# A float32 convolution with a mixing layer on one core: the last row of each output tile from four column products, two sums moved to accumulating DMA, the norms' steps listed singly

## The chip, the core and the metric

The program runs on one core of a Trainium2 chip. The core has TensorE (PE: matrix products, results in PSUM), VectorE (DVE), ScalarE (ACT), GpSimd (POOL, which here only issues DMAs that add into their destination) and SyncE (SP, which issues the plain loads and stores). The metric is the device time of one execution in microseconds; a lower time is better. A float32 product of a 128x128 weight with 512 columns shows as two matmul instructions in the profile.

## The reference

```python
def reference(x, g_pos, g_neg, bias, input_factor, output_factor, Wq, Wk, Wv, B, Wm):
    x = x + conv(groupnorm(x))        # layer 0
    x = x + mix(groupnorm(x))         # layer 1
    return x                          # x: 16 x 128 x 64 x 64, float32

def conv(x):
    v = round(clip(x * input_factor, -1, 1) * 127) / 127 * 0.6
    v = pad(swapaxes(v, -2, -1), 1)
    fv = v + 0.1 * v ** 3
    outs = [conv3x3(fv, g_pos[i] - g_neg[i]) for i in range(3)]     # 128 -> 128 channels
    adc = lambda y: clip(round(y * 0.01 * 256) / 256, -16, 16)
    m = adc(outs[2]) + 4 * adc(outs[0]) + 2 * adc(outs[1]) + adc(outs[2])
    return transpose(m * output_factor + bias)

def mix(x):                           # x as (channels, 4096)
    q, k, v = Wq @ x, Wk @ x, Wv @ x  # 64 rows each
    num, den = exp(B) @ (exp(k) * v), exp(B) @ exp(k)
    return Wm @ (q * num / den)
```

groupnorm works on 32 groups of 4 channels. The three convolutions of a 64x64 image are nearly all of the work.

## The kernel before, in words

The 16 images follow each other. For each image the convolution is done by three blocks, one for each weight set `i`, and each block by two halves: the steps of an image are numbered `.0` to `.5`, with `.0`, `.2`, `.4` the even halves (h = 0) and `.1`, `.3`, `.5` the odd ones (h = 1).

The rows of an image are cut into 16 tiles of four output rows. The 3x3 convolution over such a tile uses a short-convolution scheme down the rows with six points: each point is a fixed combination of input rows, multiplied with a fixed combination of weight rows, and the products are combined to the four output rows. Points 1 to 4 are the inner ones; points 0 and 5 touch only output row 0 and output row 3. Along a row the scheme takes pairs of columns: even columns `ev` and odd columns `od` lie side by side in a row of 66 entries.

**Inner points (class `Block`, `half`).** An even half makes points 1 and 2, an odd half points 3 and 4, with the same steps for each point (u = 0 or 1). There are four column products per point, each a 128x128 weight out of `us` with 512 columns: `q1` (weight 1 with `cs`, the sum of odd and even columns, into `pa`), an ACT copy `m1` of that to `d`, `q2` (weight 2 with `cq`, their difference, added in `pa`), an ACT copy `sd` with the sign turned from `pa` to `pb`, `q0` (weight 0 with a part of `cd`, neighbouring differences, added in `pa`), `q3` (weight 3 with another part of `cd`, added in `pb`), and an ACT copy `sA` of `pa` to `s`. VectorE then does `Bo` (s[1] = 2 d + pb), `df` (d = s[1] - s[0]) and the sum `sm`: in an even half a DMA from POOL adds s[0] into s[1]; in an odd half VectorE does it, doubled, by a custom operation (`doubled_sum`).

**Output rows (`rest`, numbered one higher than the half whose results they use).** `ma` and `mc` write output rows 1 and 2 by a custom operation that adds, bounds and rounds to int16 (`add_bounded`); `mc` reads both sums. `S0` and `S3` combine the point sums for rows 0 and 3 on VectorE. Rows 0 (even half) and 3 (odd half) also need point 0 or 5, and that goes directly: `P` is a product of weight 0 of `ud` with `sv` (sums of pairs of columns) into py[1], `bc` copies py[1] to py[0] on ACT, and `o0` and `o1` add two products each with windows of `v` into py[0] and py[1]. `tk` then adds py and the combined sums, bounded, to int16. `aA` and `aB` add the block's int16 result to `acc`: for block 0 a doubling on VectorE, for the others an adding DMA.

**Input steps of the next image** lie among these: `li`, `lj` (loads), `sx`, `sy` (sums for the norm), the norm, `n`, `cl`, `s`, `va` (quantise, clip, square, value), `cp`, `gr`, `er` (row combinations), `pa`, `pb` (inner points), `cs`, `cq`, `cd` (their columns), `p0`, `e0` (point 0 and its `sv`), `p5`, `e5` (point 5 and its `sv`). A norm is eight steps, `0 a pm b pv c l d`, with the prefix x or y; `a`, `b`, `c` and `d` are runs of small VectorE instructions on 128x1 data that are issued as a block. **Steps of the image before**: `cx` (acc to x2), `cd0x` to `cd3x` (POOL adds the input to x2), `sq`, the y norm, and the mixing layer on four chunks: `xn`, `kp`, `vp`, `qp`, `ek`, `ekv`, `dn`, `g`, `u`, `ln`, `ex`, `oa`, `ob`, `oc`, `op`, `r`, then `rd` (POOL adds x2) and `st` (store).

Every engine works its instructions strictly in the order of issue. That order is written out by hand in three lists: `FIRST` for the weights and images 0 and 1, `ORDER` for images 2 to 14, `LAST` for image 15 and the end; "+1" means the step of the image one turn before. There is no other scheduling; waits come from data alone. Weight preparation (`W0a` to `W2p`) lies in `FIRST`.

`L551` is the helper `mm` through which all convolution products go; `L558` is `add_bounded`; `L561` the doubled sum; `L588` is `Bo`, `L589` is `df`, `L597` the sum by DMA, `L615` and `L618` are `S0` and `S3`, `L624` is `bc`, `L640` the adding DMA into acc, `L697` that of the input, `L808` that of `rd`, `L509` to `L511` the columns, `L520` the pairs, `L745`, `L755`, `L767` the matmuls of the mixing layer, `L804` and `L805` are `ob` and `oc`, `L783` is the add of the last image's mixing output.

Of the kernel before, what the change touches and what calls it, by code (L numbers as in the profile page):

```python
# [39 lines left out]
    cl0+1 q01.2+1 S3.2+1 q00.2+1 sq2+1 tk.2+1 cl1+1 cd0x+1 sA1.2+1 q31.2+1 q11.3+1 s0+1 sA0.2+1  # L40
    m11.3+1 va0+1 q30.2+1 s1+1 q21.3+1 q10.3+1 sq1+1 m10.3+1 P.3+1 q20.3+1 Bo.2+1 sd1.3+1 q01.3+1
    va1+1 df.2+1 lj2+1 sq3+1 lj3+1 gr0+1 sd0.3+1 st3+1 sq0+1 q31.3+1 q30.3+1 sA1.3+1 bc.3+1 q00.3+1
    ya+1 Bo.3+1 sA0.3+1 pmy+1 yb+1 o0.3+1 n2+1 pvy+1 er0+1 st2+1 n3+1 yc+1 o1.3+1 q10.4+1 yl+1 cl2+1
    yd+1 xn0+1 q11.4+1 sm.2+1 tk.3+1 df.3+1 kp0+1 cp+1 vp0+1 m11.4+1 P.4+1 cl3+1 ma.4+1 m10.4+1
    aB.3+1 q20.4+1 ek0+1 bc.4+1 s3+1 ekv0+1 sd0.4+1 dn0+1 sm.3+1 mc.4+1 va3+1 q21.4+1 s2+1 g0+1 li0
    sx0 xn1+1 li1 S0.4+1 u0+1 ln0+1 sd1.4+1 oa0+1 x0 o0.4+1 o1.4+1 q30.4+1 ex0+1 tk.4+1 vp1+1 ob0+1
    qp0+1 kp1+1 oc0+1 aA.2+1 op0+1 va2+1 ek1+1 r0+1 ekv1+1 gr1+1 q01.4+1 sx1 q31.4+1 q00.4+1 sA0.4+1
    P.5+1 S3.4+1 sA1.4+1 bc.5+1 q10.5+1 Bo.4+1 q11.5+1 rd0+1 df.4+1 m10.5+1 er1+1 dn1+1 sy0 g1+1
    u1+1 sm.4+1 o0.5+1 o1.5+1 oa1+1 m11.5+1 st0+1 q21.5+1 aA.4+1 ln1+1 q20.5+1 pa0+1 tk.5+1 ex1+1
    sd1.5+1 pb0+1 q01.5+1 ob1+1 sd0.5+1 q00.5+1 cq0+1 xn2 qp1+1 q30.5+1 q31.5+1 oc1+1 cd0+1 cs0+1  # L50
    Bo.5+1 op1+1 sA0.5+1 kp2 r1+1 li2 vp2 q10.0 ek2 sA1.5+1 P.0 bc.0 q11.0 ekv2 pa1+1 o0.0 m11.0
# [11 lines left out]
    hs0+2 hs2+2 x0+2 hs3+2 hq0+2 hq2+2 hi+2 hq1+2 hs1+2 hq3+2 xa+2 pmx+2 xb+2 pvx+2 xc+2 xl+2 xd+2  # L63
    hn3+2 hn2+2 hc2+2 hn1+2 hn0+2 W2a+2 W1a+2 W0a+2 hc0+2 hc3+2 hc1+2 W0A+2 hr1+2 hr0+2 hv1+2 hv0+2
    gr0+2 W1A+2 er0+2 hr2+2 W0b+2 li0+1 hv2+2 W0j+2 cp+2 W0c+2 W0f+2 W0e+2 W0d+2 W0g+2 W0i+2 W0h+2
    hr3+2 li1+1 W0J+2 W0n+2 hv3+2 W0l+2 er1+2 sx0+1 W0m+2 W1c+2 x0+1 hz1+2 gr1+2 hcq1+2 W1b+2 pa1+2
    hcs1+2 hcd1+2 W2A+2 W1j+2 sx1+1 W0p+2 sy0+1 W0o+2 q10.0+1 sy1+1 li3+1 hz0+2 li2+1 W1e+2 W2b+2
    hcs0+2 W2c+2 m10.0+1 p0+1 sx3+1 pb1+2 q11.0+1 sx2+1 m11.0+1 q20.0+1 hcq0+2 W1f+2 q21.0+1 sy2+1
    cd1+2 sy3+1 hcd0+2 W1J+2 sd0.0+1 xa+1 sd1.0+1 q01.0+1 sA1.0+1 W1d+2 cs1+2 pmx+1 lj0+1 W2J+2
    q31.0+1 cq1+2 q00.0+1 q30.0+1 xb+1 pvx+1 q11.1+1 W1g+2 sA0.0+1 W1h+2 e0+1 Bo.0+1 m11.1+1 q10.1+1  # L70
    m10.1+1 W2d+2 W1i+2 W2e+2 q20.1+1 W1l+2 lj1+1 xc+1 W1m+2 W2g+2 sd0.1+1 df.0+1 q21.1+1 W2j+2 xl+1
    W0k+2 P.2+1 sm.0+1 sd1.1+1 q00.1+1 xd+1 W1n+2 q01.1+1 W1o+2 W2f+2 bc.2+1 sA0.1+1 p5+1 W2h+2
    q31.1+1 n0+1 q10.2+1 W1p+2 q30.1+1 sA1.1+1 W2i+2 cl0+1 Bo.1+1 m10.2+1 q20.2+1 W2m+2 sd0.2+1 n1+1
    o0.2+1 q11.2+1 W1k+2 q00.2+1 m11.2+1 df.1+1 sm.1+1 q30.2+1 q21.2+1 e5+1 ma.2+1 mc.2+1 S0.2+1
# [886 lines left out]
```

## Time and profile before

| | |
|---|---|
| median of 3 runs | 1575.94 us (1574.69 to 1576.45) |
| the profiled execution | 1571.91 us, its span 1570.1 us |
| instructions | 14797 |
| matmuls py<-v (points 0 and 5) | 760 instructions, 363.1 us |
| matmuls py<-sv | 192 instructions, 100.7 us |
| VectorE doubled sum 128x1024 | 48 x 1227 ns |
| POOL's sum by DMA | 48 issues, 512 KB each, 855 ns |
| DMA | 227.01 MB, 145 GB/s in the mean |

The profile's page gives the busy time of each engine over the span, a row of 40 slices with the busy share in tenths, and groups of like instructions: engine, operation, output<-inputs, shape, count, busy time, mean duration in ns, then the idle time of the engine ahead of them and what ended it. A stretch of time can be asked for by itself, with busy times of all engines. A line of waits has the waiting engine and line, what released it, the total in us, how often, and the longest.

### The profile page before, as it was taken

To read this page: it belongs to the slowest core of one execution; us is meant where nothing else is said; L and a number is where in the kernel's file an instruction comes from. 1 tells how busy PE (TensorE), PEld (TensorE's weight loads), DVE (VectorE), ACT (ScalarE), POOL (GpSimd) and SP (SyncE) were. 2 spreads that over 40 slices of the span, in tenths; PEclk is the share of its full clock that TensorE was granted. 3 is DMA by queue.
4 is the path that set the end of the run, shared out by engine and by line. 5 is a ranking of instruction groups with operands and counts; after the bars stand their busy time and mean duration, and the time that the engine had idled before them with its cause. 6 is when DMAs were issued, how large, how long until landed. Compare 5 with 4: busy or idle time off the path is not lost.

```text
span 1570.1 us, 14797 instructions
## 1 busy us (share of the span) xinstructions
PE 1481.1 (94%) x4684; PEld 564.2 (36%) x4684; DVE 1427.7 (91%) x1817; ACT 1115.6 (71%) x1859; POOL 223.1 (14%) x254
## 2 busy tenths in 40 slices
PE   1589999999999999999999999999999999999996
PEld 0233333333333433333343333433333333333331
DVE  4999999999999999999999999999999999998774
ACT  4655868687686868768686776968678686865654
POOL 2001011120201112011121201112020111201120
PEclk6799999999999999999999999999999999999997
DMA  6226478484756848476593847759385774835375
GB/s 175 78 70 132 111 165 195 107 183 134 153 147 153 209 90 181 138 155 161 131 208 98 174 137 164 173 115 219 96 168 141 165 183 108 195 87 121 81 128 154
DMA packets 67359, 227.01 MB, mean 145 GB/s; under 512 B 7632, under 2 KB 8272, under 8 KB 67280
## 3 DMA queue, kind: packets, MB, share of 16 engines
q0 software_dynamic: 38480, 125.52, 43.2%
q1 hardware_dynamic: 28512, 99.50, 18.4%
q10 hardware_dynamic: 288, 1.05, 0.2%
q8 instruction: 37, 0.61, 0.2%
q14 instruction: 42, 0.34, 0.1%
HBM read 102.30 MB, written 33.55 MB: 87 GB/s over the span
## 4 chain that ended last, share of the span: by engine, by line
PE 51%; DVE 28%; ACT 10%; issue 6%; DMA 5%; DVEq 0%; POOL 0%; ACTq 0%; POOLq 0%
PE py L551 15%; PE pa L551 14%; PE pb L551 7%; PE pz L745 5%; DVE y L558 5%; PE py L767 4%; DVE d L589 3%; DVE acc L558 3%; ACT gs L359 3%; PE py L745 3%; DVE s L615 3%; PE pz L755 2%; DMA x<-in_x_dram 2%; DVE f L502 2%; DVE s L561 2%
## 5 line engine op out<-in xcount | busy, mean ns | idle before, releaser
L551 PE MATMUL py<-v,ud 128*128 128x512 f32 x760 | 363.1, 610 | 0.0
L551 PE MATMUL pa<-cs,us 128*128 128x512 f32 x384 | 195.1, 611 | 34.2 <-DVE us L327 33.1
L551 PE MATMUL pb<-cd,us 128*128 128x512 f32 x384 | 192.7, 609 | 12.4 <-ACT pb L582 10.5
L551 PE MATMUL pa<-cq,us 128*128 128x512 f32 x384 | 197.1, 616 | 4.1 <-ACT d L580 3.9
L551 PEld LDWEIGHTS py<-v,ud 128*128 128x128 f32 x760 | 137.5, 189 | 170.4 <-issue 149.3
L551 PE MATMUL pa<-cd,us 128*128 128x512 f32 x384 | 194.6, 609 | 3.6 <-DVE x L363 2.5
L582 ACT ACTIVATE pb<-pa 128x512 f32<-128x512 f32 x192 | 112.4, 585 | 66.6 <-PE pa L551 61.6
L580 ACT ACTIVATE d<-pa 128x512 f32<-128x512 f32 x192 | 110.8, 594 | 44.1 <-PE pa L551 31.0
L808 POOL DMA_DIRECT2D xn<-x x58 | 50.2, 870 | 607.5 <-ACT xn L778 600.3
L585 ACT ACTIVATE s<-pa 128x512 f32<-128x512 f32 x192 | 111.0, 594 | 35.6 <-PE pa L551 29.8
L588 DVE SCALAR_TENSOR_TENSOR s<-d,pb 128x1024 f32<-128x1024 f32 x96 | 116.6, 1215 | 5.7 <-PE pb L551 5.6
L589 DVE TENSOR_TENSOR d<-s 128x1024 f32<-128x1024 f32 x96 | 117.1, 1220 | 2.9
L551 PEld LDWEIGHTS pa<-cs,us 128*128 128x128 f32 x384 | 68.3, 190 | 140.0 <-issue 53.4
L745 PE MATMUL pz<-xn,w 128*64 128x512 f32 x464 | 117.0, 604 | 0.0
L778 ACT ACTIVATE xn<-py,scalars 128x512 f32<-128x512 f32 x116 | 73.7, 690 | 59.9 <-PE py L767 59.9
L551 PEld LDWEIGHTS pb<-cd,us 128*128 128x128 f32 x384 | 68.3, 190 | 112.0 <-issue 71.0
L640 POOL DMA_DIRECT2D acc<-y x62 | 72.6, 1170 | 250.8 <-DVE y L558 221.1
L551 PEld LDWEIGHTS pa<-cd,us 128*128 128x128 f32 x384 | 67.9, 190 | 110.6 <-issue 71.5
L551 PEld LDWEIGHTS pa<-cq,us 128*128 128x128 f32 x384 | 66.1, 189 | 111.5 <-issue 57.8
L796 ACT ACTIVATE ek<-pz 128x512 f32<-128x512 f32 x60 | 35.8, 597 | 98.5 <-PE pz L745 86.3
L551 PE MATMUL py<-sv,ud 128*128 128x512 f32 x192 | 100.7, 607 | 1.8 <-DVE acc L558 1.6
L597 POOL DMA_DIRECT2D s<-s x48 | 41.0, 855 | 335.4 <-DVE d L589 199.9
(230 smaller groups left out, 2585.0 us busy)
## 6 DMA issues: line engine op xcount, KB each, us to landing
xc<-in_x_dram SPq DMA_DIRECT2D x121, 512.0 KB, 4.8
acc<-y POOLq DMA_DIRECT2D x62, 512.0 KB, 7.0
x<-in_x_dram POOLq DMA_DIRECT2D x60, 512.0 KB, 8.3
xn<-x POOLq DMA_DIRECT2D x58, 512.0 KB, 4.6
out_dram<-xn SPq DMA_DIRECT2D x58, 512.0 KB, 5.3
s<-s POOLq DMA_DIRECT2D x48, 512.0 KB, 5.6
gmat<-in_x_dram POOLq DMA_DIRECT2D x4, 512.0 KB, 7.0
x<-in_g_neg_dram SPq DMA_DIRECT2D x2, 576.0 KB, 11.4
```

Source lines behind the costliest of these rows:

```text
L551: pe.matmul(o if len(r.shape) == 2 else o.rearrange("p (t w) -> p t w", w=W2), w, r, start=start, stop=stop, skip_group_check=True,)
L558: dve._custom_dve(TENSOR_ADD_SAT, out=o, in0=a, in1=b, s0=QMAX, s1=-QMAX)
L580: f"m1{u}.{k}": lambda u=u, a=a: act.activation(d[:, u], a, AF.Copy),
L582: f"sd{u}.{k}": lambda a=a, b=b: act.activation(b, a, AF.Copy, scale=-1.0),
L585: f"sA{u}.{k}": lambda u=u, a=a: act.activation(s[:, u, 0], a, AF.Copy),
L588: f"Bo.{k}": lambda: dve.scalar_tensor_tensor(s[:, :, 1], d, 2.0, pb, ALU.mult, ALU.add),
L589: f"df.{k}": lambda: dve.tensor_tensor(d, s[:, 1], s[:, 0], ALU.subtract),
L640: pool.dma_start(a, y, accum_op=ALU.add)
L745: pe.matmul(self.tiles(o)[h * IC : (h + 1) * IC], w, x[:, t[0] : t[1] : t[2]], start=True, stop=True)
L767: pe.matmul(self.op[h], wm[r, :], self.o[r, :], start=True, stop=True)
L778: act.activation(g[:, t], self.tiles(self.op[h]), AF.Identity, bias=bias_sb)
L808: "rd": lambda: pool.dma_start(self.r, self.x2, accum_op=ALU.add),
```

## The change

Row 3 (point 5, odd halves) no longer goes through `v`, `sv` and `ud`. Point 5 gets column sums and differences like the inner points, as fifth entries of `cs`, `cq` and `cd` (new steps `cs2`, `cq2`, `cd2`; `e5` is gone), and fifth weights in `us`. The products are now `P` (weight 1 with `cs` into py[0]), a VectorE step `tq` (t = 2 py[0] + t, where t is the combined sum for row 3), `o0` (weight 2 with `cq`, added in py[0]), `bc` (ACT, py[1] = -py[0]) and `o1` (weights 0 and 3 with two parts of `cd`, added in py[0] and py[1]): four products in place of five. Row 0 stays as it was.

The odd sum `sm` becomes the same adding DMA as the even one. The factor 2 that it carried goes into the weights of points 3 and 4 (1/3 and 1/6 for 1/6 and 1/12), and the odd difference is halved in a custom operation (`half_difference`).

Each norm step of several instructions is split in the lists (`ya` into `ya0` to `ya4`, and so on); the instructions are the same. The three lists are written anew. In the steady order the input's adding DMAs stand as `cd0x` ... `sm.1`, `cd3x`, `cd1x`, `cd2x` (before: `cd2x`, `cd1x`, `cd3x`, `cd0x`), and POOL's further order is `sm.2`, `sm.3`, `aA.2`, `aA.4`, `aB.3`, `rd0`, `sm.4`, `aB.5`, `rd1`, `sm.5`, `aA.0`, `rd2`, `sm.0`, `aB.1`, `rd3`.

```diff
-    v = buf("v", 2, T, RW)
-    cd = buf("cd", 4, T, 2 * W2)
-    cs = buf("cs", 4, T * W2)
-    cq = buf("cq", 4, T * W2)
-    sv = buf("sv", 2, T * W2)
+    v = buf("v", T, RW)
+    cd = buf("cd", 5, T, 2 * W2)
+    cs = buf("cs", 5, T * W2)
+    cq = buf("cq", 5, T * W2)
+    sv = buf("sv", T * W2)
...
-    us = [buf(f"us_{i}", 4, 4, C) for i in range(3)]
-    ud = [buf(f"ud_{i}", 2, 5, C) for i in range(3)]
+    us = [buf(f"us_{i}", 5, 4, C) for i in range(3)]
+    ud = [buf(f"ud_{i}", 5, C) for i in range(3)]
...
-                "g": lambda: copy(r[:, 0], g1, AF.Copy, scale=1.0 / 6.0),
-                "h": lambda: stt(u[:, 2, 0:3], r[:, 2], 1.0 / 12.0, r[:, 0], ALU.mult, ALU.add),
-                "i": lambda: stt(u[:, 3, 0:3], r[:, 2], 1.0 / 12.0, r[:, 0], ALU.mult, ALU.subtract),
+                "g": lambda: copy(r[:, 0], g1, AF.Copy, scale=1.0 / 3.0),
+                "h": lambda: stt(u[:, 2, 0:3], r[:, 2], 1.0 / 6.0, r[:, 0], ALU.mult, ALU.add),
+                "i": lambda: stt(u[:, 3, 0:3], r[:, 2], 1.0 / 6.0, r[:, 0], ALU.mult, ALU.subtract),
+                "j": lambda: copy(u[:, 4, 0:3], g2, AF.Copy),
...
+        def last_row(self):
+            z = f[:, 0:T]
+            o = {"p5": lambda: self.point(5, z)}
+            for k, g in self.columns(slice(4, 5), z).items():
+                o[f"{k}2"] = g
+            return o
...
+    def half_difference(o, a, b):
+        dve._custom_dve(TENSOR_TENSOR_REDUCE_SUB_MAX, out=o, in0=a, in1=b, s0=0.0, s1=0.5)
...
-        def sum(self, s, h):
-            if h:
-                doubled_sum(s[:, 1], s[:, 1], s[:, 0])
-            else:
-                pool.dma_start(s[:, 1], s[:, 0], accum_op=ALU.add)
+        def sum(self, s):
+            pool.dma_start(s[:, 1], s[:, 0], accum_op=ALU.add)
+
+        def difference(self, s, h):
+            d = self.d[h]
+            if h:
+                half_difference(d, s[:, 1], s[:, 0])
+            else:
+                dve.tensor_tensor(d, s[:, 1], s[:, 0], ALU.subtract)
...
+        def extra(self):
+            return us[self.i][:, 4]
+
+        def first(self, y):
+            mm(y[:, 0], self.extra()[:, 1], cs[:, 4], True, True)
+
+        def odd(self, y):
+            t = self.d[0][:, 1]
+            dve.scalar_tensor_tensor(t, y[:, 0], 2.0, t, ALU.mult, ALU.add)
+
+        def second(self, y):
+            mm(y[:, 0], self.extra()[:, 2], cq[:, 4], False, True)
+
+        def turn(self, y):
+            act.activation(y[:, 1], y[:, 0], AF.Copy, scale=-1.0)
+
+        def third(self, y):
+            mm(y[:, 0], self.extra()[:, 0], cd[:, 4, :, W2 : 2 * W2], False, True)
+            mm(y[:, 1], self.extra()[:, 3], cd[:, 4, :, 0:W2], False, True)
...
+            if h:
+                o |= {
+                    f"P.{k}": lambda: self.first(py),
+                    f"tq.{k}": lambda: self.odd(py),
+                    f"o0.{k}": lambda: self.second(py),
+                    f"bc.{k}": lambda: self.turn(py),
+                    f"o1.{k}": lambda: self.third(py),
+                }
...
         def operations(self, k):
-            return {
-                f"{k}0": self.shift, f"{k}a": self.begin, f"pm{k}": self.means, f"{k}b": self.squares,
-                f"pv{k}": self.variances, f"{k}c": self.guess, f"{k}l": self.root, f"{k}d": self.finish,
-            }
+            o = {f"pm{k}": self.means, f"pv{k}": self.variances, f"{k}l": self.root}
+            for e, steps in zip("0abcd", (self.shift, self.begin, self.squares, self.guess, self.finish)):
+                o |= {f"{k}{e}{n}": f for n, f in enumerate(steps())}
+            return o
```

Two stretches of the new steady list, around the sums of the odd halves and the new step:

```
    Bo.1 df.1 xl cq2 bc.2 q11.2 cx2 cx3 cd0x xd0 q10.2 xd1 cd2 m10.2 ma.2 o0.2
    y01+1 m11.2+1 S3.2+1 q20.2+1 sm.1+1 q21.2+1 n1+1 o1.2+1 cd3x+1 n0+1 sd0.2+1 sd1.2+1 q00.2+1
    cl1+1 cl0+1 s1+1 mc.2+1 S0.2+1 q01.2+1 cd1x+1 q30.2+1 q31.2+1 s0+1 sA1.2+1 cd2x+1 va1+1 sA0.2+1
...
    qp0+1 oc0+1 vp1+1 op0+1 sA0.4+1 va3+1 ek1+1 aB.3+1 q30.4+1 q01.4+1 r0+1 P.5+1 rd0+1 ekv1+1 gr1+1
    tq.5+1 sA1.4+1 sy0 dn1+1 Bo.4+1 q10.5+1 o0.5+1 li2 q11.5+1 g1+1 bc.5+1 oa1+1 m11.5+1 er1+1
```

## The prediction

> **What bounds the kernel.** I read the page first, then busy times in stretches of one image, then the groups of instructions and the waits of VectorE inside ten such stretches, then single matmuls in time.
>
> ```profile
> span 1570.1 us, 14797 instructions
> ...
> PE 1481.1 (94%) x4684; PEld 564.2 (36%) x4684; DVE 1427.7 (91%) x1817; ACT 1115.6 (71%) x1859; POOL 223.1 (14%) x254
> ...
> PE   1589999999999999999999999999999999999996
> ...
> PEclk6799999999999999999999999999999999999997
> ```
>
> TensorE is full from the fourth slice on, at full clock. In the chain of waits a piece of eight py matmuls recurs at 384.77, 477.19, 570.07 and 662.46: one image takes 92.5 us. Four such stretches:
>
> ```profile
> core 0: us, PE busy (x) PEld busy (x) DVE busy (x) ACT busy (x) POOL busy (x), PEclk, DMA share, GB/s
> 235.00:327.50 92.50, 91.46 (x293) 34.76 (x292) 87.03 (x111) 68.91 (x116) 13.58 (x15) 1.00 0.66 153
> 327.50:420.00 92.50, 91.42 (x293) 34.84 (x293) 87.05 (x111) 69.11 (x116) 13.58 (x15) 1.00 0.65 153
> ...
> sum 370.00, PE 365.72 PEld 139.05 DVE 348.07 ACT 276.14 POOL 54.32; mean PE 91.43 PEld 34.76 DVE 87.02 ACT 69.04 POOL 13.58
> ```
>
> TensorE has 1.1 us of idle time per image: it is the bound. VectorE stands idle 5.5 us per image and is the next bound. ACT (69.0) and POOL (13.6) are far off. How VectorE's idle time ends, over ten images (235 to 1160 us):
>
> ```profile
> DVE ekv L805 <- PE py L745: 18.0, 10, 1.8
> DVE y L558 <- PE py L551: 9.6, 10, 1.0
> DVE x L392 <- PE pz L387: 5.6, 10, 0.6
> DVE y L402 <- ACT y L398: 2.8, 10, 0.4
> ```
>
> The first two (with 1.2 us of another line, 2.9 us per image) are waits for large matmuls: VectorE is ahead there, and they go if TensorE gets faster. The remaining 2.6 us per image (norm steps, 1.4 us of small gaps) are VectorE's own.
>
> **Part 1, one matmul less per odd half.** `P`, `o0`, `o1` of an odd half have 1+2+2 products before and 1+1+2 after. A float32 product is two instructions (the row of py<-v has 479 in ten images: 3 blocks x 2 halves x 4 products x 2 = 48 each). Their price is start to start, not the mean:
>
> ```profile
> 720.63 1.13 PE L551 MATMUL pa<-cq,us 128*128 128x512 f32 x2
> 721.60 1.02 PE L551 MATMUL pa<-cs,us 128*128 128x512 f32 x2
> 722.46 1.02 PE L551 MATMUL py<-sv,ud 128*128 128x512 f32 x2
> ```
>
> 721.60 to 722.46 is 0.86 us for a product that follows at once; 720.63 to 721.60 is 0.97 for one with a wait in front, 0.11 more. So 48 blocks x 0.86 = **-41.3 us** (2.58 per image). The new step `tq` stands between `P` and `o0`, so `o0` gets a wait that it did not have: 48 x 0.11 = **+5.3** (between 0, if the wait is over already, and 5.3). Queued behind a late `o0` is all of TensorE. The issue order puts two products between `P.3` and `o0.3` (1.72 us) for the 0.7 us of `tq.3`; ahead of `tq.5` stands `gr1` on VectorE (2.6 us), and TensorE has `dn1` and `q10.5` to do (about 1.05 + 0.86). That cover holds only while TensorE is behind VectorE; if not, about 1 us per image is lost there. `bc` stays one ACT copy 128x512 (586 ns), now with the sign turned; ACT does not change.
>
> **Part 2, VectorE per image.** Its rows, over the same ten images:
>
> ```profile
> L561 DVE CUSTOM_DVE_ANT_0 s<-s 128x1024 f32<-128x1024 f32 x30 | 36.8, 1228 | 0.7
> L510 DVE TENSOR_TENSOR cq<-f 128x1024 f32<-128x1024 f32 x20 | 24.4, 1220 | 0.0
> L520 DVE TENSOR_TENSOR sv<-v 128x512 f32<-128x512 f32 x20 | 13.7, 684 | 0.0
> ```
>
> Start to start, an instruction takes some 0.08 us less than its mean (1.14, 1.13, 0.60). Gone: three doubled sums, -3.43, and one `e5`, -0.60. New: `cs2` and `cq2`, 2 x 0.60; `cd2` (128x1024), 1.13; three `tq`. No row before is a multiply-add of 128x512 with one PSUM input inside the loop; the row L805 (a PSUM input, 685 ns) gives 0.61 and L783 (scalar_tensor_tensor from PSUM, 746 ns) 0.70: 1.8 to 2.1, I take 1.85 since most 128x512 rows lie at 0.69. Sum +0.15. The halved difference is another custom operation; its nearest row is L561 (1.228 against 1.220 for the plain difference), the far one L558 (1.36): 0 to +0.4, I take 0 as shape and type are L561's. The norms' steps are the same instructions, single in the order: 0, with up to 1.4 us per image of small gaps that other work can now fill. VectorE's floor is 87.0 + 0.15 + 2.6 = **89.8 us** per image, against TensorE's 92.5 - 2.58 + 0.33 = **90.25**. The two nearly meet.
>
> **Part 3, the odd sums as DMA.** The rows of the even ones:
>
> ```profile
> L597 POOL DMA_DIRECT2D s<-s x30: 841/848/872, 261.9 to 1158.5; - x30
> ...
> DMA to landing us min/median/max: 4.7/5.8/8.3
> ```
>
> 48 more issues of 0.85 us on POOL (13.6 to 16.1 us per image: hidden by POOL's idle time, at no cost unless the queue stands still). By the queue's rows (43.2% of the span for 125.52 MB) an accumulating transfer of 0.52 MB takes 2.83 us of all 16 engines: three more per image lift the DMA share from 0.66 to about 0.77. What is late next is `mc`, which needs both sums. A sum is issued 0.3 us after the difference ends (663.30 to 663.60). By the new order VectorE has between `df` and `mc`: 5.2 us (`df.1` to `mc.2`), 6.05 (`df.3`), 6.4 (`df.5`). At a landing of 4.7 nothing waits; at 5.8 the waits are 0.9 + 0.05 + 0 = 1.0 us per image; at 8.3 they are 3.4 + 2.55 + 2.2 = 8.1. Behind `mc` on VectorE stand `S0`, `tk` and the rest of the block, and TensorE waits for those through py. Taking the median, VectorE needs 90.8 less what the single norm steps fill; I take 90.6 for the period, 0.35 over TensorE's floor, x 14 images = **+5** (0 to +14, at one us per image).
>
> In the POOL queue `sm.1` now stands behind `cd0x`, `sm.3` behind `sm.2`, `sm.5` behind `aB.5` and `rd1`; `cd1x` to `cd3x` stand behind `sm.1`, `aA.2` behind `sm.3`, `aA.0` behind `sm.5`. Each has its input ready some us earlier, and x<-in_x_dram lands after 8.3 us in the median, so `sm.1` beside `cd0x` is the likeliest to be late. On SP the same twelve transfers per image change places (`li1`, `li2` earlier, `st2` before `st3`); SP waits hundreds of us for its inputs, so that costs nothing.
>
> [...]
>
> **Part 4, start and end.** The first convolution matmul starts at 51.95, after a wait of 33.09 us for VectorE. The new order puts before it `pb1`, `p0`, `hz0` (3 x 1.17), `cd1` (2.2), `cq1` (1.13), `e0` (0.6), `W1c`, `W0k` and wider weight sums (together 1.2), and `hcd1` (1.13) after it: 7.5 us later. But between 52 and 133 us TensorE idles another 9.0 us (93 - 72.06 - 11.95) because VectorE (91.5 of 93) feeds it too slowly, and that work is now done earlier: I take **+3** (-1.5 to +7.5). In the tail `tmc` waits for the last DMA sum: 4.2 us of VectorE work lie over 6.1, a wait of 1.9 in place of a 1.15 us sum, and `tP1`, `tq0`, `tp0`, `tb0`, `tp1` are a longer chain: **+2** (0 to +4).
>
> **Sum.** -41.3 + 5.3 + 3 + 5 + 2 = -26.0 on the span of 1570.1: 1544.1. The profiled execution took 1571.91 (1.8 around the span), 4.0 below the median 1575.94. So 1544.1 + 5.8 = **1550 us**.
>
> **Rivals.** *A, TensorE keeps all of it* (20%): no wait shows and the start costs nothing, 1570.1 - 41.3 + 5.8 = 1535 to 1541. For it: TensorE is kept to 1.1 us of idle time per image today. Against: VectorE would have to be 97% busy. *B, VectorE becomes the bound with the idle time that it has* (13%): 87.0 + 0.15 + 5.5 = 92.65 per image, +0.15 x 14 = +2, the ends' +5 paid by the 2 x 2.58 of the two images left over: 1578, from 1566 to 1582. For it: VectorE already fills 94%. Against: 2.9 of the 5.5 us are waits for matmuls. *C, late sums, slower* (16%): at `mc`, if odd sums land after 7.3 us in the mean, the waits are 2.4 + 1.55 + 1.2 = 5.1 us, less the 1.4 that fills gaps: 93.5 per image, +1.0 x 14 = +14: 1590. It decides from 92.5 - 89.8 = 2.7 us of waiting per image, a mean landing of about 6.5 us, or 7 if gaps fill; at 8.3 throughout (89.8 + 8.1 - 1.4 = 96.5) it is 1632. For it: the median 5.8 is not far, and the DMA share rises. Against: the accumulating xn<-x lands after 4.5 to 5.2 us. That the products do not drop I exclude: the odd half's code issues four.
>
> **Chances.** My forecast 51%, with its own range 1541 to 1566 (the terms at their upper ends: -41.3 + 5.3 + 7.5 + 14 + 4 = -10.5, 1565); A 20, B 13, C 16. The range 1534 to 1577 leaves out C and a part of B. A change under 0.2% (3 us) can't be told from none here: faster 51 + 20 + 7 = 78%, same 4 (B's middle), slower 16 + 2 = 18.
>
> **What would show it.** Right: py<-v down from 760 to about 384 instructions and a group of 128x512 products on cs, cq, cd in py; a period near 90.6; VectorE at 96% or more; DMA share near 0.77; s<-s x96 with a median landing near 6. Wrong: VectorE's longest wait is `mc` for the sum (C), or TensorE idles for `tq` by more than 1 us per image, or the first convolution matmul is past 60 us and the idle time after it stays at 9 us.

## The result and the profile after

The changed kernel takes 1593.7 us (median of 4 runs, 1591.1 to 1594.5) beside 1575.3 for the kernel before on the same chip: a ratio of 1.0117, 95% interval 1.0104 to 1.0129. It is slower by 18 us where 26 us less were predicted. Three sums per image go to DMA, `sm.1`, `sm.3` and `sm.5`, not two as the title has it: the group s<-s has 96 issues in place of 48.

The page of the changed kernel, cut to the lines that answer to those shown of before:

```profile
span 1592.8 us, 14803 instructions
...
PE 1452.6 (91%) x4586; PEld 543.8 (34%) x4586; DVE 1427.4 (90%) x1849; ACT 1126.2 (71%) x1854; POOL 264.4 (17%) x302
...
PE   1798999999989999998999999999998989999995
...
PE 47%; DMA 21%; DVE 18%; ACT 6%; issue 6%; POOL 1%; DVEq 0%; ACTq 0%; SPq 0%; POOLq 0%
...
L610 POOL DMA_DIRECT2D s<-s x96 | 82.0, 855 | 614.5 <-DVE d L617 306.9
...
L567 PE MATMUL py<-v,ud 128*128 128x512 f32 x376 | 176.7, 604 | 0.2 <-ACT py L664 0.2
...
s<-s POOLq DMA_DIRECT2D x96, 512.0 KB, 5.3
...
x<-in_x_dram POOLq DMA_DIRECT2D x60, 512.0 KB, 9.5
```

TensorE has lost the work that the change takes away (28.5 us less busy, py<-v from 760 to 376 instructions), and the span is longer all the same: it now waits. Eights stand in its row of slices, and of the chain that ended last 21% is DMA (5% before).

Where in the span? One small matmul of the y norm comes twice per image, at fixed places, and dates the images. Its group in the kernel before and in the changed one (duration min/median/max, then first to last start):

```profile
L378 PE MATMUL pz<-y,grp x30: 167/250/271, 172.1 to 1468.7; 128*128 128x1 f32 x30
```

```profile
L386 PE MATMUL pz<-y,grp x30: 167/250/271, 167.6 to 1493.7; 128*128 128x1 f32 x30
```

From first to last lie 14 images: 92.61 us each before, 94.72 after, +29.5 in all. What lies ahead of the first and behind the last is 273.5 before and 266.7 after, -6.8. Together +22.7, the difference of the spans. So the whole loss is in the steady stretch, and I look at 12 whole images of it; first the kernel before, then the changed one (start and end, length, busy us of PE, PEld, VectorE, ACT and POOL, then clock, DMA share and GB/s):

```profile
264.70:1376.00 1111.30, 1097.93 (x3505) 417.69 (x3503) 1044.71 (x1317) 829.43 (x1379) 163.01 (x180) 1.00 0.66 153
```

```profile
262.30:1398.90 1136.60, 1076.49 (x3427) 402.78 (x3427) 1043.20 (x1339) 836.92 (x1378) 193.91 (x216) 1.00 0.74 166
```

Divided by 12: TensorE is busy 91.49 us per image before and 89.71 after, VectorE 87.06 and 86.93. Both engines do about what was forecast. The waits in the same stretches (waiting engine and line, releaser, us in total, times, longest), of TensorE before, where two smaller lines add 1.8 us (in the kernel before, L582 is the copy sd):

```profile
PE pb L551 <- ACT pb L582: 9.2, 12, 0.8
```

and after, of TensorE. In the changed kernel L567 is `mm`, L574 `add_bounded`, L596, L598 and L601 are the copies m1, sd and sA, L367 is the squares `sq`, and L800 the products q, k and v of the mixing layer; in the runs further down the numbers are a few lines higher.

```profile
PE py L800 <- DVE y L574: 19.7, 12, 2.5
PE pa L567 <- ACT pb L598: 14.7, 12, 2.6
PE pa L567 <- ACT s L601: 8.3, 11, 1.1
PE pa L567 <- ACT d L596: 7.2, 12, 1.0
PE py L800 <- DVE x L391: 6.4, 12, 0.5
```

TensorE waits 0.92 us per image before and 4.93 after (with 2.9 us in all of two smaller lines). 89.71 + 4.93 = 94.64, the period but for 0.08. What its releasers wait for themselves, VectorE first, then ACT:

```profile
DVE y L574 <- DMA s<-s: 21.5, 12, 2.6
...
DVE acc L574 <- DMA s<-s: 8.9, 12, 1.2
```

```profile
ACT gs L367 <- DMA x<-in_x_dram: 34.8, 33, 3.2
```

Two paths lead there from transfers. First, VectorE's `mc.4` waits 1.8 us per image for the sum `sm.3`, and the product `qp0` (L800) needs what stands behind it: 1.6 us. Second, ACT waits 2.9 us per image (0.4 before) in the squares `sq` for the input that POOL adds to x2; the copies m1 and sd stand behind them in ACT's order, and TensorE waits 1.8 us for those (L596, L598). The chain of waits goes through that transfer, in time order:

```profile
621.84 0.88 POOL x L752 x2
...
622.92 15.78 DMA x<-in_x_dram
...
638.78 0.83 ACT gs L367
```

An input add that lands after 15.78 us. What else ran then shows in POOL's timeline, and in the busy time of the DMA engines in stretches of 4 us (DMA share and GB/s stand last in the lines):

```profile
616.93 0.86 POOL L752 DMA_DIRECT2D x<-in_x_dram  x1 [1.70 <-ACT x L749]
620.46 0.84 POOL L610 DMA_DIRECT2D s<-s  x1 [2.67 <-DVE d L577]
621.84 2.65 POOL L752 DMA_DIRECT2D x<-in_x_dram  x3 [0.54 <-ACT x L749]
```

```profile
620.00:624.00 4.00, 4.00 (x10) 1.53 (x9) 3.97 (x8) 4.00 (x8) 3.00 (x4) 1.00 1.03 195
...
632.00:636.00 4.00, 2.84 (x6) 1.06 (x6) 3.12 (x5) 2.02 (x4) 0.85 (x1) 1.00 1.07 277
636.00:640.00 4.00, 3.29 (x8) 1.43 (x8) 2.08 (x2) 3.60 (x9) 0.00 (x0) 1.00 1.04 259
640.00:644.00 4.00, 3.75 (x12) 1.80 (x12) 3.04 (x13) 3.13 (x7) 0.00 (x0) 1.00 0.12 26
```

Where the image changes, the DMA engines are full from 620 to 640 (share 0.99 to 1.07), and nearly empty after. In the kernel before they are full there for 16 us, from 712 to 728 (1.01 to 1.06), without `sm.1`. That is one transfer more, 2.8 us of all 16 engines. Whether it is what makes the others late, the first experiment answers.

### The profile page after: what moved, and what is told of

Read it like the earlier page. It is cut to its first block, busy times and chain, and to the rows that moved or that the text cites. A ratio compares the mean times of both kernels' runs of the same rounds, so it can differ in the third digit from the quotient of the medians.

```text
span 1592.8 us, 14803 instructions
## 1 busy us (share of the span) xinstructions
PE 1452.6 (91%) x4586; PEld 543.8 (34%) x4586; DVE 1427.4 (90%) x1849; ACT 1126.2 (71%) x1854; POOL 264.4 (17%) x302
## 4 chain that ended last, share of the span: by engine, by line
PE 47%; DMA 21%; DVE 18%; ACT 6%; issue 6%; POOL 1%; DVEq 0%; ACTq 0%; SPq 0%; POOLq 0%
PE pa L567 13%; DMA x<-in_x_dram 13%; PE py L567 12%; DMA s<-s 7%; PE pb L567 6%; PE pz L800 4%; DVE y L574 4%; PE py L800 4%; PE pz L810 3%; PE py L822 3%; DVE cd L522 2%; DVE f L513 2%; DVE s L635 1%; DVE s L604 1%; ACT gs L367 1%
## 5 line engine op out<-in xcount | busy, mean ns | idle before, releaser
L567 PE MATMUL pa<-cd,us 128*128 128x512 f32 x384 | 195.9, 606 | 16.8 <-ACT pb L598 16.7
L567 PE MATMUL pa<-cs,us 128*128 128x512 f32 x384 | 192.4, 608 | 20.2 <-ACT s L601 11.8
L567 PE MATMUL pa<-cq,us 128*128 128x512 f32 x384 | 199.9, 622 | 11.5 <-ACT d L596 9.2
L567 PE MATMUL pb<-cd,us 128*128 128x512 f32 x384 | 198.9, 614 | 1.0 <-ACT pb L598 1.0
L610 POOL DMA_DIRECT2D s<-s x96 | 82.0, 855 | 614.5 <-DVE d L617 306.9
L567 PE MATMUL py<-v,ud 128*128 128x512 f32 x376 | 176.7, 604 | 0.2 <-ACT py L664 0.2
L598 ACT ACTIVATE pb<-pa 128x512 f32<-128x512 f32 x192 | 112.2, 584 | 59.9 <-PE pa L567 56.7
L601 ACT ACTIVATE s<-pa 128x512 f32<-128x512 f32 x192 | 110.7, 592 | 40.0 <-PE pa L567 21.6
L596 ACT ACTIVATE d<-pa 128x512 f32<-128x512 f32 x192 | 107.5, 589 | 20.6 <-PE pa L567 16.3
L800 PE MATMUL pz<-xn,w 128*64 128x512 f32 x464 | 117.9, 609 | 0.0
L680 POOL DMA_DIRECT2D acc<-y x62 | 63.4, 1023 | 309.0 <-DVE y L574 238.7
L567 PEld LDWEIGHTS pa<-cs,us 128*128 128x128 f32 x384 | 69.9, 191 | 119.4 <-issue 66.1
L567 PEld LDWEIGHTS pa<-cd,us 128*128 128x128 f32 x384 | 67.5, 189 | 115.0 <-ACT pb L598 64.0
L567 PEld LDWEIGHTS pa<-cq,us 128*128 128x128 f32 x384 | 64.3, 189 | 123.0 <-ACT d L596 71.4
L567 PEld LDWEIGHTS py<-v,ud 128*128 128x128 f32 x376 | 71.4, 191 | 93.1 <-issue 91.2
L567 PEld LDWEIGHTS pb<-cd,us 128*128 128x128 f32 x384 | 66.9, 190 | 102.5 <-issue 81.3
L367 ACT ACTIVATE gs<-x,y 128x1024 int16<-128x1024 f32 x60 | 68.7, 1145 | 38.9 <-DMA x<-in_x_dram 38.9
L567 PE MATMUL py<-cd,us 128*128 128x512 f32 x192 | 94.3, 613 | 0.0
```

The source lines that it names most:

```text
L367: act.activation(o, a, AF.Square, bias=self.sh, scale=UNIT, accum_out=self.sums[:, 1, q : q + 1])
L567: pe.matmul(o if len(r.shape) == 2 else o.rearrange("p (t w) -> p t w", w=W2), w, r, start=start, stop=stop, skip_group_check=True,)
L596: f"m1{u}.{k}": lambda u=u, a=a: act.activation(d[:, u], a, AF.Copy),
L598: f"sd{u}.{k}": lambda a=a, b=b: act.activation(b, a, AF.Copy, scale=-1.0),
L601: f"sA{u}.{k}": lambda u=u, a=a: act.activation(s[:, u, 0], a, AF.Copy),
L610: pool.dma_start(s[:, 1], s[:, 0], accum_op=ALU.add)
```

## The experiments

The theory after this reading (DMA in the first expectations, TRANSFERS in later ones): the transfers of `sm.1` and `sm.3` cost what they delay. Its rivals: the longer chain of the last row or the new order costs it (CHAIN), or VectorE has become the bound. One table ahead of the single runs. Each ratio is to the kernel before on the same chip (1572.7 to 1575.5 us), so kernels that ran on different chips are best compared by ratios; period from the y norm's matmul (14 images), busy times and TensorE's waits over 12 images, us per image:

| kernel | time, us | ratio to before | period | TensorE busy | its waits | VectorE busy |
|---|---|---|---|---|---|---|
| before | 1575.3 | 1 | 92.61 | 91.49 | 0.92 | 87.06 |
| changed | 1593.7 | 1.0117 | 94.72 | 89.71 | 4.93 | 86.93 |
| e1 sm.1 on VectorE | 1566.2 | 0.9938 | 92.73 | 89.35 | 3.26 | 88.11 |
| e2 sm.3 on VectorE | 1585.1 | 1.0062 | 93.89 | 89.69 | 4.09 | 88.20 |
| e9 sm.1, sm.3 on VectorE | 1559.9 | 0.9918 | 91.94 | 89.37 | 2.45 | 89.32 |
| e3 sm.1, sm.3, sm.5 on VectorE | 1575.7 | 1.0002 | 93.17 | 89.69 | 3.38 | 90.45 |
| e10 changed, P twice | 1624.9 | 1.0334 | 96.41 | 92.09 | 4.21 | 87.29 |
| e11 e3, P twice | 1611.8 | 1.0248 | 95.46 | 92.07 | 3.28 | 90.61 |
| e6 input adds ahead of sm.1 | 1641.3 | 1.0420 | 97.61 | 91.19 | 6.32 | 86.89 |
| e12 squares later | 1619.7 | 1.0296 | 96.34 | 91.22 | 5.14 | 87.15 |
| e15 e9, cd2 later | 1591.3 | 1.0109 | 94.19 | 90.21 | 3.85 | 89.16 |
| e18 e15, s0 later | 1562.7 | 0.9928 | 92.14 | 89.56 | 2.41 | 89.19 |

In every row TensorE's work and its waits add up to the period within 0.2 us.

**Sums back on VectorE (e1, e2, e3, e9).** The same edit with other numbers of the sum:

```
-        pool.dma_start(s[:, 1], s[:, 0], accum_op=ALU.add)
+        if k in (1,):
+            dve.tensor_tensor(s[:, 1], s[:, 1], s[:, 0], ALU.add)
+        else:
+            pool.dma_start(s[:, 1], s[:, 0], accum_op=ALU.add)
```

> Of the changed kernel, only sm.1 goes back to VectorE (a plain 128x1024 add). Theory DMA (the 16 DMA engines are full around the input adds, sm.1 makes them land later, and ACT stands at the squares): 2.8 us of transfers leave the full stretch, the slowest input add lands after about 12.5 us in place of 15.5, ACT's wait for x falls from 3.0 to under 1 us per image, VectorE gains 1.1 us of work; the period falls by about 2 us, time 1560 to 1575 us. Theory CHAIN (the longer chain of row 3 and the new order cost the time, DMAs only fill waits that are there anyway): no gain, 1594 to 1610 us.

> Of the changed kernel, only sm.3 goes back to VectorE. Theory DMA: the wait of mc.4 for its sum (1.7 us per image) and TensorE's wait behind it (1.5 us) go, VectorE gains 1.1 us of work, the wait at the squares (3.0 us) stays: 1572 to 1584 us. Theory CHAIN: 1594 to 1610 us.

> All three odd sums go back to VectorE, row 3 and the order stay as changed. Theory DMA: both waits go, VectorE has 3.4 us more and is the bound at some 93 us per image: 1565 to 1585 us. Theory CHAIN: VectorE's 3.4 us come on top, 1600 to 1640 us.

> The odd sums sm.1 and sm.3 are adds on VectorE again (128x1024), sm.5 stays an adding DMA; nothing else differs from the changed kernel. Theory TRANSFERS (each sum's transfer costs where it lands): sm.1 alone gave 27.5 us back and sm.3 alone 8.6 us, so both give up to 36, 1558 us, less what VectorE's 1.13 us more per image takes now that it comes near its bound: 1557 to 1568. Theory VECTORE (what is left after sm.1 is VectorE's own limit, so a further add on it costs): 1568 to 1576, no better than with sm.1 alone (1566).

`sm.1` alone gives 27.5 us back (1566.2, interval of the ratio 0.9923 to 0.9953). Over 12 images ACT's wait falls from 34.8 to this, in the kernel e1:

```profile
ACT gs L367 <- DMA x<-in_x_dram: 1.6, 3, 0.9
```

TensorE's waits for the copies m1 and sd fall with it, from 21.9 to 0.8 us. The input adds land earlier again; from issue to landing over eight images, in the kernel before, the changed one and e1:

```profile
DMA to landing us min/median/max: 6.1/8.2/12.2
```

```profile
DMA to landing us min/median/max: 6.2/10.4/15.8
```

```profile
DMA to landing us min/median/max: 5.7/8.2/13.8
```

They are not issued any faster: in the image shown POOL issues the four adds from 616.93 to 624.49 in the changed kernel, and in the same image of e1 from 609.32 to 616.96, 7.6 us in both. So the loss is not that POOL stood at `sm.1` with the adds behind it; with the same places in the queue and one transfer less they land sooner.

`sm.3` alone gives 8.6 us; the wait of `mc.4` goes and that of the squares stays (35.4). That is just above what the first theory expected and below what CHAIN did. Both together give 33.8 (31 by the ratios), and e9, at 0.9918 (0.9902 to 0.9933), is the fastest kernel of this study, as the first theory expected (1557 to 1568). But `sm.5`, which nobody waited for, costs some 16 us (13 by the ratios) when it too goes back: the period grows by 1.23, and the add's time on VectorE is 1.13. So it is paid about in full, though VectorE stands idle 2.7 us per image in e3.

**The products done twice (e10, e11).** Is the saved product worth its 0.86 us?

```
             mm(y[:, 0], self.extra()[:, 1], cs[:, 4], True, True)
+            mm(y[:, 0], self.extra()[:, 1], cs[:, 4], True, True)
```

> The first product of each new last row (P in the odd halves) is done twice, the second time over the first one, so that TensorE has five products per odd half again, as before the change: 48 products of 0.86 us, 41.3 us more TensorE work. The output stays the same. Theory REPAID (the four products did save their 41 us, and the waits cost some 59 us more elsewhere): TensorE's work and its waits add up, 1628 to 1640 us. Theory SWALLOWED (TensorE only waits in the time that it saved; the period of 94.6 us is set by transfers and by ACT's and VectorE's order): the extra products fill idle time of TensorE (4.9 us per image), 1594 to 1612 us.

> All three odd sums on VectorE and P done twice in the odd halves: TensorE's and VectorE's work as before the change, but in the new order and with the new last row. Theory VECTORE (with the sums on VectorE, its 90.4 us of 93 set the period and the products do not): the extra 41 us of TensorE work fill most of its idle time, 1577 to 1592 us. Theory TENSORE (the products still set the period there, and the new order costs 41 us that the saved products pay): 1605 to 1620 us.

Three products more make TensorE 2.38 us busier per image (0.79 each). In e11 the period grows by 2.29, nearly all of it, and the time (1611.8) lies where TENSORE had it: e3 is not bound by VectorE, as I had read it, and theory VECTORE falls. In e10 31 us (34 by the ratios) of 41 appear, between the two theories: TensorE's waits shrink by 0.7 us per image. So the saved products did count. What is odd is that VectorE's work counts too. TensorE's longest waits over 12 images in e3, and in e11:

```profile
PE pa L567 <- ACT s L601: 12.0, 12, 1.1
PE pz L813 <- DVE ekv L855: 10.4, 12, 0.9
PE pa L567 <- ACT pb L598: 6.5, 14, 0.5
PE py L803 <- DVE x L391: 6.4, 12, 0.5
```

```profile
PE pa L567 <- ACT s L601: 12.0, 12, 1.1
PE pz L814 <- DVE ekv L856: 10.4, 12, 0.9
PE py L804 <- DVE x L391: 6.3, 12, 0.5
PE pa L567 <- ACT pb L598: 6.0, 13, 0.5
```

2.3 us per image more for VectorE to catch up, and the waits stay (3.38 and 3.28 us per image). They stand at fixed places of the list, in stretches that `P` does not lie in. I read this so, without a run that shows it alone: there another engine is the bound for the moment, and elsewhere TensorE is. An image then costs the sum over its stretches of the slowest engine in each, not the larger of two sums over the whole image.

**Which transfer goes first (e6, e8), and the covers (e5, e7).**

In e6 and e8 the input adds change places around `sm.1`, and the squares stand in the order 0 to 3:

```
- cd0x ... sm.1+1 ... cd3x+1 ... cd1x+1 ... cd2x+1
+ cd1x+1 ... sm.1+1 ... cd2x+1 ... cd3x+1
```

There `cd0x` stays at the end of the turn, ahead of `cd1x`. In e5, e7 and e8 work is put ahead of the waits for `sm.3`:

```
- mc.4+1 ... tk.4+1 va2+1 qp0+1 ... q30.4+1 q01.4+1
+ va2+1 mc.4+1 ... tk.4+1 q30.4+1 q01.4+1 qp0+1
```

e7 has the second edit alone, e8 both. e5 is e1 with the second edit, and `sm.1` just ahead of `mc.2`.

> The changed kernel with all sums by DMA; only POOL's order is cd0x, cd1x, sm.1, cd2x, cd3x (it was cd0x, sm.1, cd3x, cd1x, cd2x) and the squares follow as 0, 1, 2, 3. Theory DMA with the queue's order as its cause: cd1x goes out some 4 us and cd2x 2 us earlier, ACT's wait for x falls from 3.0 to about 1 us per image, 1565 to 1584 us. Theory DMA with the transfers' amount alone as its cause (the engines are full, whatever the order): 1588 to 1596 us.

> The changed kernel with all sums by DMA; only q30.4 and q01.4 stand ahead of qp0 and va2 ahead of mc.4. If TensorE's wait at qp0 (1.5 us per image) is head-of-line blocking by the late sum sm.3, it goes: 1568 to 1582 us. If the wait moves on: 1588 to 1596 us.

> The edits of e6 and e7 together, all sums by DMA. If the two losses are independent and both lie in the order: 1545 to 1565 us. If either lies in the amount of transfers: 1570 to 1585 us.

> e1 (sm.1 on VectorE) with three steps moved in the steady list: sm.1 behind the clips cl1 and cl0, and, to cover the wait of mc.4, q30.4 and q01.4 ahead of qp0 on TensorE and va2 ahead of mc.4 on VectorE. If the rest of the loss is the late sum sm.3 standing at the head of VectorE and TensorE, the 1.5 us per image that TensorE waits at qp0 and about half of the 1.1 us at q1.3 go: 1537 to 1552 us. If the waits only move to the next step: 1560 to 1568 us.

Both expectations failed for e6 (1641.3) and e8 (1642.1). With two input adds ahead of it, ACT's wait for the input goes, and `sm.1` is late instead. In e6 VectorE, and TensorE behind it, wait (12 images):

```profile
DVE acc L578 <- DMA s<-s: 51.9, 12, 5.1
```

```profile
PE pa L571 <- ACT s L605: 50.7, 11, 5.0
```

POOL does not issue `sm.1` late: in one image of e6 it waits 1.56 us for VectorE ahead of it (2.67 in the changed kernel, at 620.46), and the transfer goes out at 641.57; it is the landing that is late, by up to the 5.1 us that VectorE waits for it. No free place was found in the full stretch: one transfer's gain is another's delay, and here `mc.2` waits 4.3 us per image where the squares had waited 2.9. But only 1.39 of the 2.89 us by which e6's period is longer than the changed kernel's are waits; 1.48 are a longer busy time of TensorE for the same work, at a granted clock of 0.97 where the changed kernel has 1.00 (last section). The covers (e7, 1593.6) took the wait of `qp0` from 19.7 to 0.6 us, and 16.4 us came at `P.5`, which then waits for the copy `r0`; nothing was won, nor in e5 (1567.7). Both times are in the ranges for waits that only move.

**Is it ACT's order (e12)?**

```
- sq3+1 m10.3+1 m11.3+1 sq1+1 ... sd0.3+1 sq0+1 sq2+1
+ m10.3+1 m11.3+1 ... sd0.3+1 sq3+1 sq1+1 sq0+1 sq2+1
```

> The squares sq3 and sq1, which wait on ACT for the input's adding DMAs, stand behind the copies m1 and sd of step .3 in the order, with sq0 and sq2; no transfer and no instruction is changed. Theory ACT ORDER (the late input adds cost time because the squares block ACT's copies, for which TensorE waits): most of the 27 us that removing sm.1 gave come back, 1568 to 1583 us. Theory NORM (the late input adds cost time through the norm and the mixing layer behind them): no gain, 1588 to 1600 us.

Neither range: 1619.7, slower by 26. TensorE's waits are about the same in sum (5.14 us per image, 4.93 in the changed kernel), so nothing came back, as theory NORM had it. What is slower is TensorE's work, 91.22 us for 89.71, at a granted clock of 0.98 for 1.00 (last section): 1.51 of the 1.62 us that the period grew. The copies are free now, and the norm that needs the squares is late: TensorE waits for it with the y norm's first matmul in e12, 2.65 us per image.

```profile
PE pz L390 <- DVE y L383: 31.8, 12, 4.2
```

So the late input adds are paid on either path. That their lateness is the cost, not the place of the squares, is what e1 shows.

**A price for transfers in the kernel before (e4).** Three adding DMAs more per image in the kernel before, behind the doubled sums; each adds s[0] to itself after its last use.

```
                 doubled_sum(s[:, 1], s[:, 1], s[:, 0])
+                pool.dma_start(s[:, 0], s[:, 0], accum_op=ALU.add)
```

> The kernel before, with three more adding DMAs of 512 KB per image on POOL after the odd sums (each adds a dead half of s onto itself, and no step waits for it but the next writer of that half). Theory DMA: the input adds land 2 to 3 us later, ACT waits for x about 2 us per image where it had 0.5, and TensorE's 1.1 us of idle time grow: 1585 to 1605 us. Theory CHAIN: extra transfers alone cost nothing, 1573 to 1579 us.

Missed by all: 1785.5. POOL stands at the new DMA (L596) until the doubled sum is done, and what is behind it in POOL's order waits as well:

```profile
523.00 0.85 POOL L596 DMA_DIRECT2D s<-s  x1 [17.83 <-ACT pb L582]
```

```profile
557.90 0.85 POOL L596 DMA_DIRECT2D s<-s  x1 [15.72 <-ACT xc L430]
558.44 1.18 POOL L809 DMA_DIRECT2D xn<-x  x1
```

The releasers in these lines are inferred; the doubled sums end on VectorE at 522.45 and 557.37, some 0.5 us ahead of the issues. After the second one the next DMA of POOL's order goes out at once, so it had been ready. It is no price of a transfer; it shows what a place in POOL's queue can cost (13%, a part of it by the granted clock, 0.934 in the mean where the kernel before has 0.979).

**The order, or the last row (e13)?** The new last row with all odd sums on VectorE, in the three lists of the kernel before. In this kernel `hz1` stands ahead of `W0o` and `W0p` and overwrites what they read, so that the weights 1 and 2 of block 0 are other numbers; the work is the same.

> The new last row with its four products, the split norms and the new weights, all three odd sums as adds on VectorE, but in the three lists of the kernel before: every step stands where it stood, the columns cs2, cq2, cd2 stand from the place of e5 on, and tq, o0 and bc of the odd halves lie between P and o1. Beside it stands the same kernel in the new lists, at 1575.7 us, whose TensorE waits 3.3 us per image (0.9 before the change). Theory ORDER (the new list costs the waits): TensorE's work of about 89.5 us and 0.9 to 1.8 us of waits give 90.4 to 91.3 per image, 1540 to 1560 us. Theory LAST ROW (the waits come with the four products and tq, or VectorE with its 90.4 us per image sets the period in any order): 1568 to 1585 us.

1651.9 us, far above both. Its period is 96.39. TensorE waits 5.6 us per image there at other places (most of it for the copies m1, sd, sA and the y norm), VectorE is busy 90.9. The old list was made for the old last row; so this does not tell what the new list costs; that stays open.

**Moving single steps in the best version (e14 to e18).** In e9 VectorE works almost without a gap ahead of `S0.2` (19.47 of the 20 us from 603 to 623), and TensorE waits 1.0 us per image for the copy sA behind it. I moved what could stand later:

```
- q10.2 xd1 cd2 m10.2 ma.2 o0.2
+ q10.2 xd1 m10.2 ma.2 o0.2
...
- mc.2+1 S0.2+1 q01.2+1
+ mc.2+1 S0.2+1 cd2+1 q01.2+1
```

This is e15 (made from e9) and e17 (made from the changed kernel). e16 is e15 with `sm.3` behind `ekv0`; e18 is e15 with `s0` behind `sA0.2` and `m10.3` ahead of `sq3`; e14 is e9 with only those places of `s0` and `sm.3`:

```
- s0+1 sA1.2+1 cd2x+1 va1+1 sA0.2+1
+ sA1.2+1 cd2x+1 va1+1 sA0.2+1 s0+1
...
- sm.3+1 aA.2+1 P.4+1 ekv0+1
+ aA.2+1 P.4+1 ekv0+1 sm.3+1
```

> As the kernel with sm.1 and sm.3 on VectorE (1559.9 us), with two steps of the new list moved: s0 (a square on ACT) behind the copy sA0.2, and sm.3 (an add on VectorE) behind ekv0. They stand ahead of two of the three waits that TensorE has left there: 1.0 us per image for sA ahead of q10.3 and 0.87 for ekv0 ahead of dn0. Theory ORDER (TensorE's period is its work and these local waits, and a wait goes when what is ahead of it is moved): 1.9 us per image come back, 1530 to 1540 us. Theory MOVES ON (the waits turn up at the next place, since VectorE or ACT sets the period): 1550 to 1564 us.

> As the kernel with sm.1 and sm.3 on VectorE (1559.9 us), with one step moved: cd2 (128x1024, 1.13 us on VectorE, which o1.3 needs some 15 us later) from ahead of mc.2 to behind S0.2. VectorE works without a gap there for 20 us, and the copy sA.2 and with it TensorE wait for S0.2: 1.0 us per image. Theory LOCAL (the period is TensorE's work and what it loses in stretches where VectorE is full for the moment, not the larger of the two sums over an image): the wait goes and 0.9 us per image come back, 1543 to 1551 us. Theory LOAD (VectorE's 89.3 us of work per image set the period; its order does not matter): 1556 to 1564 us.

> As the one before, with sm.3 (an add on VectorE) behind ekv0, for which TensorE waits 0.87 us per image. In the earlier run with this move beside that of s0 the wait for ekv0 went, but others of 0.3 to 0.6 us came, and the time rose by 8 us. LOCAL: 1535 to 1545 us if the move of s0 did that harm. LOAD: 1560 us or more.

> The changed kernel itself, all sums by DMA, with cd2 moved in the same way. Theory TRANSFERS (there the full DMA engines around the input adds, by the squares and the norm, and the late sum sm.3 set TensorE's waits): little or nothing, 1586 to 1596 us. LOCAL: 1575 to 1583 us.

> As the kernel with sm.1 and sm.3 on VectorE and cd2 behind S0.2 (1591.3 us), with s0 behind the copy sA0.2 and m10.3 ahead of sq3. There s0 (a square on ACT that writes the rows of f which cd2 still reads) waited 2.5 us per image for cd2, and the copy sA.2 stood behind it, so TensorE waited 2.4 us per image where it had waited 1.0. Theory LOCAL: with s0 out of the way S0.2 comes 1.1 us earlier and the wait of 1.0 goes; the copies m1 then cost up to 0.5 as in the run with s0 moved: 1545 to 1556 us. Theory LOAD (VectorE's and ACT's work in that stretch set its length in any order): 1557 to 1568 us.

Measured: 1567.8, 1591.3, 1590.9, 1608.8 and 1562.7, none better than e9's 1559.9. e16 and e18 lie in LOAD's ranges, e14 is 4 us above that of MOVES ON, and e15 and e17 are slower than both their theories. In e15 I had overlooked that `s0` on ACT writes the rows of `f` that `cd2` still reads. In e15, TensorE and ACT over 12 images:

```profile
PE pa L572 <- ACT s L606: 28.5, 11, 2.6
```

```profile
ACT f L480 <- DVE cd L527: 29.5, 11, 2.7
```

e16 and e17 have the same. In e15 TensorE's work takes longer too, 90.21 us per image for e9's 89.37, at a clock of 0.99 for 1.00. In e18 that is out of the way, and the wait is halved, but another takes what it gave:

```profile
PE pz L818 <- DVE ekv L860: 10.4, 12, 0.9
PE py L808 <- DVE x L396: 6.4, 12, 0.5
PE pa L572 <- ACT d L601: 6.0, 12, 0.7
PE pa L572 <- ACT s L606: 5.9, 11, 0.6
```

2.41 us per image in all, as 2.45 in e9. In e14 and e16 the wait for ekv0 goes in the same way, and waits for `xn` and `tk.4` of 10.0 us in 12 images come for its 10.4. So no single move helped, and the theory that a place in the list is the cost (LOCAL) was not borne out; that the stretch is full on ACT, VectorE and TensorE together was only argued.

## Why the prediction was wrong

- **Part 1, right in kind, 0.5 us per image short.** Four products per odd half run, worth 0.79 us each by e10 and e11 where I took 0.86. TensorE's busy time falls by 1.78 per image, not by 2.58 - 0.33 = 2.25. About 0.28 of the 0.47 is the clock (an estimate: half of 2 x 3.41 us, divided by 12): in the 12 images it is twice at 0.50 for 3.41 us (from 1133.16 and from 1208.25 on), after waits of 2.45 and 2.62 us. The rest I put down to more products with a wait in front, which no run shows alone; in e9, with fewer waits, the fall is 2.12. `tq` itself cost nothing visible: no line of TensorE's waits names it.
- **Part 2, right.** VectorE's work changed by -0.13 us per image (forecast +0.15). POOL's rose to 16.2 (forecast 16.1).
- **Part 3, the step that failed.** "Taking the median, VectorE needs 90.8 less what the single norm steps fill; I take 90.6 for the period, 0.35 over TensorE's floor, x 14 images = +5". The period is 94.72, 4.47 over that floor of 90.25: +63 where +5 was taken. Three things are in it. *One median for three places:* the sums land after 5.3 us in the median, even earlier than the 5.8 taken, but `mc.4` waits 1.8 us per image (I had 0.05), since `sm.3` lands late (the one issued at 647.10 landed at 654.74, after 7.6 us; that the loads and the store beside it cause this is a reading, for the DMA share there is 0.79 from 644 to 648 and 0.82 from 648 to 652, not 1.0); `mc.2` waits 0.74 (0.9 forecast) and `mc.0` not at all. *The other transfers:* I asked when `sm.1` would land beside `cd0x`, not what `sm.1` does to the four input adds. Those had no term at all, and by e1 they are 27.5 of the 58 us that this part missed (with `mc.2`'s own wait in it). *Two floors compared as sums:* with `sm.1` and `sm.3` eased (e9) TensorE still waits 2.45 us per image, 1.5 more than before. I had counted the 2.9 us that VectorE waited for matmuls as free reserve; e9, e3 and e11 show that both sums count: 1.13 us more for VectorE and 2.38 more for TensorE each lengthen the period nearly in full. That an image has stretches for each engine is my reading of it.
- **Part 4, better than forecast.** The work outside the 14 images fell by 6.8 us; the forecast there was +5 with the products' -5.2 for two images. TensorE's first convolution matmul starts at 42.44 in place of 51.95, since the new list puts a product of row 0 first; the first inner product starts at 51.16, so the delay of 7.5 us did not come.
- **The rivals.** C, slower by late sums, has the right side and nearly the number (1590), but no run shows its mean landing of 7.3 us (over eight images the sums land after 4.5 to 7.7 us, 5.5 in the median), and its place is right only for the smaller part: `mc` waits 2.5 us per image, not 5.1, and VectorE, which it made the bound, stands idle 7.8 us of an image. The larger part comes by the input adds. A's and B's signs do not show: DMA is in the chain, VectorE's busy share fell.

What stays open: what the last 1.5 us per image of e9's waits come from (the new list, or VectorE with 2.6 us of idle time in place of 5.5), since e13 did not answer and the moves of single steps only shifted them. The lists of waits tell where two of them enter: 0.87 us for `ekv` stand in e2, e3 and e9, where the add `sm.3` is ahead of `ekv0` on VectorE, and not in the changed kernel or e1; 0.53 us for a step of the x norm (L391) stand in the runs of the new lists (changed, e1 to e3, e5 to e12 and e14 to e18), and neither before nor in e13.

## What to carry to other kernels

Work moved from a busy engine to a DMA was not priced here by that transfer's landing alone (`sm.1`, for which `mc.2` waits 0.74 us per image, cost 27.5 us by e1): look at the DMA share in stretches of a few us where it will run, and if it is at 1.0 already, price every transfer in that stretch and who waits for it in order. A sum that shows a wait behind it may go back to the engine, and one that nobody waits for may stay: here that choice (sm.5 by DMA, sm.1 and sm.3 on VectorE) beat both all and none. And two engines that both work nearly all the time did not give a period of the larger one here (in e9 they are busy 89.37 and 89.32 us of a period of 91.94): compare them by stretches, and let the range hold the waits of both.

## What the hardware showed

**After a short wait the granted clock was halved.** In e6 and e12 TensorE is busy 91.2 us per image for the work that takes 89.7 in the changed kernel; the granted clock over the 12 images is 0.97 and 0.98 there, 1.00 in the changed kernel. In e12, after a wait of 2.46 us that ends at 652.58, the busy times by stretches (the clock is the last but two):

```profile
650.00:653.00 3.00, 0.54 (x4) 0.42 (x4) 0.77 (x5) 2.97 (x7) 0.00 (x0) 0.97 0.76 152
653.00:656.00 3.00, 3.00 (x6) 1.45 (x7) 1.34 (x7) 1.82 (x4) 0.00 (x0) 0.50 0.18 26
656.00:659.00 3.00, 3.00 (x8) 1.24 (x6) 2.55 (x5) 1.44 (x3) 0.00 (x0) 0.96 0.85 236
```

The granted clock is halved for 3 us (0.50 from 653 to 656), and a product takes 2.05 us there where the ones from 646.45 to 649.11 take 1.02 to 1.10. What stands ahead of it is the wait of 2.46 us and a tiny matmul of 0.38 us; that the wait is the cause is my reading. The length of the wait does not decide it alone: in e15 one of 2.59 us that ends at 634.15 left the clock at 1.00, and the shorter one of 2.45 us in the changed kernel, which ends at 1132.77, was followed by a clock of 0.50 from 1133.16 to 1136.57. In e6 the longer busy time is half of what the period grew over the changed kernel's, in e12 nearly all of it.

**The same transfer, 6 to 16 us.** Over eight images the input adds, 512 KB each, land after 6.1 to 12.2 us before (median 8.2) and 6.2 to 15.8 after (10.4), and the sums after 4.5 to 7.7. That all transfers draw on the same 16 engines there, each at the cost of the others, is my reading of the shares of 1.0 in the full stretch (0.99 to 1.07 in the changed kernel, 1.01 to 1.06 before) and of e6, where the wait of the squares went and `mc.2` waits 4.3 us per image; no run shows it by itself. The issues did not get longer with their number: a sum's issue on POOL takes 855 ns in the mean with 96 of them as with 48, beside a VectorE that is busy 90% and 91% of the span.
